# A selective scan on one core: the B product of four states at a time, decays in SBUF, and one session of activation functions per pass

## The chip, the cores and the metric

The kernel runs on one core of a Trainium2 chip. The core has five engines that run side by side, each working through its own queue in order: PE (TensorE, matrix products into PSUM), DVE (VectorE), ACT (ScalarE, activation functions), POOL (GpSimd) and SP (SyncE, which here issues DMAs). SBUF is the working memory, PSUM the memory that PE writes into; PSUM has eight banks of 512 fp32 values per partition. The metric is the device time of one execution in microseconds (us). It was 14339.09 us before the change (median of three runs, 14334.58 to 14341.66).

## The reference

The input is 16 images of 64 x 64 positions with 128 channels. Two layers follow each other, each as `x = x + layer(group_norm(x))`. Layer 0 is a two-dimensional LSTM over the diagonals of the image. Layer 1, in which the change lies, is a selective scan (Mamba) over the 4096 positions of each image, once forward and once backward, with the two results added:

```python
xz = x @ in_w.T
xc, z = jnp.split(xz, 2, axis=-1)             # 256 inner channels each
...
xc = jax.nn.silu(...)                         # after a causal convolution of 4 taps
dbl = xc @ x_w.T
dt, Bm, Cm = jnp.split(dbl, [DT_RANK, DT_RANK + D_STATE], axis=-1)
dt = jax.nn.softplus(dt @ dt_w.T + dt_b)
dA = jnp.exp(dt[..., None] * A)               # decay, 16 states per channel
dBx = dt[..., None] * Bm[:, :, None, :] * xc[..., None]
def step(h, inp):
    dA_t, dBx_t, C_t = inp
    h = dA_t * h + dBx_t
    y = jnp.einsum('bds,bs->bd', h, C_t)
    return (h, y)
...
y = ys + xc * D
y = y * jax.nn.silu(z)
return y @ out_w.T
```

For every inner channel and each of 16 states there is a recurrence over time, `h = decay * h + drive`, where the drive is `dt * x * B`; the output is the sum over the states of `h * C`.

## The kernel before

**Tiling.** Layer 1 works in 256 passes: 16 images, and for each 8 chunks of 512 positions forward and the same 8 backward. In a pass the 256 inner channels are two halves (`h` = 0, 1) of 128 partitions, and there are 16 states (`s`), so a pass has 32 recurrences of 512 steps. Each is one `tensor_tensor_scan` on DVE (line 1277, `scan`), with the decay as one tensor input, the drive as the other, and the last column of the chunk before (`carry`) as its start.

**Two ways for the states.** States 0 to 7 (kind "X" in the planner) get their drive from POOL: `drive` multiplies `dtx` = dt * x by a row of B that a DMA has spread over all partitions (`br`), for two states at once, into a tile `group` in SBUF that holds four states interleaved. The scan writes its result in place. PE then transposes the group (`turned`), ACT copies it out of PSUM (`turned_take`, into `ht`), and PE weighs it with C by a matrix product (`weigh`, with four column groups of 32). States 8 to 15 (kind "R") get their drive from PE: `drive_rows` multiplies the transposed `dtx` (`dtxt`) by a matrix `d` in which the B values of the states lie on a diagonal. That matrix is put together in DRAM by `scatter` and loaded by `spread`. The product of two states fills the two PSUM banks of the tile "pair", and the scan reads it from there and writes to `hst` in SBUF. POOL multiplies `hst` by a row of C (`out_of`, line 1300, into `hc`), and PE adds the result into the PSUM tile `py` (`sums`).

**Decays.** `decay` (line 1217) is an Exp on ACT. For the R states it writes to `das`, a tile of SBUF for two states; for the X states it writes to one of four PSUM banks, tag "bank0" to "bank3", which it shares with small products ("misc"). The planner limits each of the two uses to two banks at a time.

**PSUM.** The eight banks are: four of "bank", two of "pair" (also used by `dtproj`, the product for dt), two of "py".

**Activation functions.** Exp, Silu and Softplus need different tables on ACT, and a change of function needs a table load. In a pass ACT leaves Exp twice: for a session of Silu (of pass i + 2, and the gate of pass i in the backward passes) and for a session of Softplus (of pass i + 1). In a session no decay is issued between its activations.

**Order.** The order of all instructions is fixed ahead of the launch: `order_of_issue` lists every step with its engine, its cost (`COST`), what it must follow, what buffers it takes (`RINGS`) and a priority (`URGENCY`), and `simulate` plays this through and puts out one order. Each engine then runs its part in that order; waits between engines are by semaphores. `ORDER` says how scans of X groups (digits) and R pairs (letters) follow each other: "00a00b11c11d..." is two scans of group 0, two of pair a, two of group 0, two of pair b, and so on.

Of the kernel before, what the change touches and what calls it, by code (L numbers as in the profile page):

```python
# [8 lines left out]
F32 = mybir.dt.float32  # L9
# [5 lines left out]
P = 128  # L15
# [21 lines left out]
GX = 4  # L37
TB = P // GX
NX = 8
NG, NR = NX // GX, (NS - NX) // 2  # L40
WD = T + P
ORDER = ("00a00b11c11d22e22f33g33h", "00a00b11c11d22e22f33g33h")


def units_of(order):

    count = {}
    for x in order:
# [3 lines left out]
        else:  # L52
# [4 lines left out]
    "bank": 4, "pair": 1, "py": 1, "das": 3, "dg": 3, "group": 3, "cd": 2, "ht": 6, "hst": 3, "hc": 4,  # L57
    "br": 3, "cr": 2, "xc": 2, "dt": 2, "dtx": 2, "dtxt": 2, "dbl": 2, "z": 1, "y": 1,
# [4 lines left out]
    "conv": 0.865, "gate": 0.87, "silu": 0.62, "softplus": 0.65, "gate_take": 0.6, "dtproj": 1.07,  # L63
    "xproj": 1.0, "xproj_take": 0.4, "times": 2.34,
    "turn": 0.47, "turn_take": 0.47, "decay": 0.62, "drive": 2.34, "drive_rows": 1.08,
    "scan": 1.18, "keep": 0.6, "keep_group": 0.6, "out": 2.34, "sums": 0.88, "skip": 0.44,
    "turned": 0.44, "turned_take": 0.47, "weigh": 1.08,
    "again": 0.88, "finish": 1.0, "finish_last": 1.2, "back": 0.47, "back_take": 0.47,
    "project": 0.95, "store_take": 0.6, "residual": 0.6, "read_load": 0.6, "read_turn": 0.47,
    "read_take": 0.5, "read_stats": 0.62, "normal": 3.0, "normalise": 0.75, "spread": 0.6, "rows": 1.2,  # L70
# [4 lines left out]
LIMIT = {"misc": 2, "bank": 2}  # L75
AHEAD = 3
ROW = 0.9
# [4 lines left out]
        {(0, 0): -5.27, (0, 1): -61.96, (0, 2): -1.51, (0, 3): -31.9, (1, 0): -36.36, (1, 1): -34.22, (1,  # L82
         2): -4.82, (1, 3): -3.48},
        {(0, 0): -13, (0, 1): -15.31, (0, 2): -17.47, (0, 3): -12.25, (1, 0): -17.78, (1, 1): -17.99, (1,
         2): -18.46, (1, 3): -13.31},
    ),
    "xproj": (
        {(): 55.58},
        {(): 50.35},
    ),  # L90
    "xproj_take": (
        {(): -34.19},
        {(): -67.81},
    ),
    "rows": (
        {(): 14.85},
        {(): 29.35},
    ),
    "dtproj": (
        {(): 21.81},  # L100
        {(): 49.19},
    ),
    "times": (
        {(): -216.85},
        {(): -50.5},
    ),
    "turn": (
        {(0,): -139.83, (1,): -112.3},
        {(0,): 38.45, (1,): 39.27},
    ),  # L110
    "turn_take": (
        {(0,): -82.61, (1,): -85.08},
        {(0,): -121.61, (1,): -124.32},
    ),
    "skip": (
        {(0,): -30.72, (1,): -29.27, (2,): -28.89, (3,): -30.37},
        {(0,): -31.71, (1,): -38.35, (2,): -27.4, (3,): -32.33},
    ),
    "spread": (
        {("b", 0): 48.76, ("d", 0): -27.02, ("c", 0): -72.82, ("b", 1): -39.91, ("k", 0): 25.29, ("d",  # L120
         1): -25.84, ("c", 1): 91.24, ("b", 2): 203.69, ("d", 2): 42.8, ("c", 2): -76.57, ("b", 3): 83.9,
         ("k", 1): -178.37, ("d", 3): 47.98, ("c", 3): -120.82},
        {("b", 0): -102.07, ("d", 0): 101.39, ("c", 0): -127.37, ("b", 1): 201.12, ("k", 0): -7.75, ("d",
         1): -16.19, ("c", 1): 237.63, ("b", 2): 27.93, ("d", 2): 187.94, ("c", 2): 178.25, ("b", 3):
         59.58, ("k", 1): 33.49, ("d", 3): -19.86, ("c", 3): 49.53},
    ),
    "drive": (
        {(0, 0): -37.87, (1, 0): -232.55, (0, 1): 70.61, (1, 1): 81.52, (2, 0): 92.85, (3, 0): -81.77,
         (2, 1): 90.65, (3, 1): -60.19},
        {(0, 0): 71.45, (1, 0): 100.65, (0, 1): 69.84, (1, 1): 238.34, (2, 0): -85.16, (3, 0): 16.29, (2,  # L130
         1): 152.24, (3, 1): 151.41},
    ),
    "decay": (
        {(0, 0): -100.09, (1, 0): -113.38, (8, 0): -17.88, (9, 0): -17.98, (2, 0): 115.94, (3, 0):
         -173.37, (8, 1): 117.83, (9, 1): 117.76, (0, 1): 117.57, (1, 1): -199.13, (10, 0): -76.99, (11,
         0): -4.35, (2, 1): -207.87, (3, 1): -174.5, (10, 1): -57.93, (11, 1): 144.9, (4, 0): -62.8, (5,
         0): 9.44, (12, 0): -249.7, (13, 0): -4.82, (6, 0): -90.12, (7, 0): -89, (12, 1): 112.66, (13,
         1): -89.33, (4, 1): -92.07, (5, 1): -92.07, (14, 0): -87.45, (15, 0): -79.99, (6, 1): -83.78,
         (7, 1): -65.02, (14, 1): -92.12, (15, 1): -92.18},
        {(0, 0): -107.74, (1, 0): 78.08, (8, 0): 64.21, (9, 0): 60.4, (2, 0): 66.94, (3, 0): -168.8, (8,  # L140
         1): -38.24, (9, 1): 83.45, (0, 1): -165.22, (1, 1): -93.49, (10, 0): -104.1, (11, 0): 17.18, (2,
         1): 7.23, (3, 1): -108.8, (10, 1): 238.21, (11, 1): -142.57, (4, 0): 16.12, (5, 0): 79.59, (12,
         0): 187.77, (13, 0): -57.05, (6, 0): 11.51, (7, 0): -45.79, (12, 1): 48.63, (13, 1): 3.55, (4,
         1): 76.92, (5, 1): 79.55, (14, 0): 84.29, (15, 0): -45.77, (6, 1): 8.28, (7, 1): 1.52, (14, 1):
         78.29, (15, 1): 80.29},
    ),
    "scan": (
        {(0, 0): -191.9, (1, 0): -180.93, (8, 0): 59.29, (9, 0): 58.95, (2, 0): 47.07, (3, 0): 1.2, (8,
         1): 43.31, (9, 1): 42.72, (0, 1): 139.84, (1, 1): 85.46, (10, 0): 88.15, (11, 0): -220.11, (2,
         1): 67.38, (3, 1): 69.08, (10, 1): 3.2, (11, 1): -48.38, (4, 0): -148.38, (5, 0): -142.6, (12,  # L150
         0): -158.76, (13, 0): -146.42, (6, 0): -147.36, (7, 0): -134.74, (12, 1): -175.53, (13, 1):
         71.17, (4, 1): 33.69, (5, 1): 137.17, (14, 0): 92.55, (15, 0): 96.04, (6, 1): 94.32, (7, 1):
         102.78, (14, 1): 86.19, (15, 1): 71.66},
        {(0, 0): -48.3, (1, 0): -50.57, (8, 0): -47.99, (9, 0): -52.26, (2, 0): -45.52, (3, 0): -48.53,
         (8, 1): -128.37, (9, 1): -157.26, (0, 1): -63.33, (1, 1): -80.02, (10, 0): -74.43, (11, 0):
         -109.52, (2, 1): -66.59, (3, 1): -80.53, (10, 1): 9.22, (11, 1): -125.5, (4, 0): -93.94, (5, 0):
         3.58, (12, 0): 2.78, (13, 0): -27.3, (6, 0): 34.58, (7, 0): 18.59, (12, 1): 6.11, (13, 1):
         12.29, (4, 1): 11.19, (5, 1): 13.36, (14, 0): 20.12, (15, 0): 47.53, (6, 1): 63.73, (7, 1):
         24.81, (14, 1): -31.39, (15, 1): -31.89},
    ),  # L160
    "scatter": (
        {("d", 0): -127.75, ("k", 0): -48.3, ("d", 1): 125.59, ("d", 2): 30.9, ("k", 1): -11.07, ("d",
         3): 59.14},
        {("d", 0): -28.6, ("k", 0): -67.41, ("d", 1): -108.16, ("d", 2): -133.73, ("k", 1): -94.37, ("d",
         3): -129.9},
    ),
    "drive_rows": (
        {(0, 0): 26.17, (0, 1): -3.25, (1, 0): -50.93, (1, 1): -31.58, (2, 0): -0.9, (2, 1): 17.32, (3,
         0): 80.19, (3, 1): -2.75},
        {(0, 0): 33.35, (0, 1): 87.4, (1, 0): -31.34, (1, 1): 14.65, (2, 0): 33.69, (2, 1): 74.37, (3,  # L170
         0): 149.93, (3, 1): -83.5},
    ),
    "keep": (
        {(0, 0): -27.42, (0, 1): -63.13, (1, 0): -50.2, (1, 1): 26.86, (2, 0): 11.68, (2, 1): 92.99, (3,
         0): -130.98, (3, 1): -233.75},
        {(0, 0): -235.44, (0, 1): 51.58, (1, 0): 122.52, (1, 1): 76.67, (2, 0): 102.66, (2, 1): -10.28,
         (3, 0): 48.92, (3, 1): -97.12},
    ),
    "out_of": (
        {(0, 0): 59.79, (0, 1): 61.42, (1, 0): -184.01, (1, 1): -237.54, (2, 0): -19.88, (2, 1): -39.04,  # L180
         (3, 0): 15.92, (3, 1): -83.32},
        {(0, 0): 46.75, (0, 1): 3.87, (1, 0): 82.21, (1, 1): 206.76, (2, 0): 148, (2, 1): -37.11, (3, 0):
         94.4, (3, 1): 76.66},
    ),
    "sums": (
        {(0, 0): 41.95, (0, 1): 68.64, (1, 0): 88.31, (1, 1): 50.57, (2, 0): 73.72, (2, 1): 76.8, (3, 0):
         -112.6, (3, 1): 161.24},
        {(0, 0): 22.75, (0, 1): 60.23, (1, 0): 33.88, (1, 1): 40.44, (2, 0): 217.19, (2, 1): 108.14, (3,
         0): 79.41, (3, 1): 83.91},
    ),  # L190
    "keep_group": (
        {(0, 0): -57.74, (0, 1): 14.03, (1, 0): 44.89, (1, 1): 61.89},
        {(0, 0): -23.9, (0, 1): -25.46, (1, 0): -99.2, (1, 1): -131.55},
    ),
    "turned": (
        {(0, 0, 0): 7.49, (0, 0, 1): -48.32, (0, 0, 2): -49.41, (0, 0, 3): 27.18, (0, 1, 0): 30.12, (0,
         1, 1): 23.21, (0, 1, 2): 38.21, (0, 1, 3): 37.84, (1, 0, 0): 60.1, (1, 0, 1): 19.71, (1, 0, 2):
         91.82, (1, 0, 3): -28.89, (1, 1, 0): 50.64, (1, 1, 1): 50.33, (1, 1, 2): 64.2, (1, 1, 3): 154.68},
# [16 lines left out]
        {(0, 0): 103.15, (0, 1): 79.93, (1, 0): 103.9, (1, 1): 79.84},  # L215
    ),
    "finish": (
        {(): -99.64},
        {(): -37.02},
    ),  # L220
    "spill": (
# [1250 lines left out]
```

## Time and profile before

| | |
|---|---|
| median of 3 runs | 14339.09 us |
| the profiled execution | 14002.73 us |
| its span, first to last instruction | 14000.9 us |
| mean granted PE clock | 0.973 |
| busy, share of the span: PE | 13085.1 us, 93% |
| PE's weight loads | 10060.3 us, 72% |
| DVE | 11100.8 us, 79% |
| ACT | 10791.8 us, 77% |
| POOL | 10438.0 us, 75% |
| moved by DMA | 1936.50 MB, mean 138 GB/s |

All times of single rows come from the profiled execution, which was shorter than the median of the runs by 336 us. The span has two parts: layer 0, some 1.6 ms at the beginning, in which POOL does little, and layer 1, which repeats its pass to the end. The page also divides the span into 40 slices and shows the busy share of each engine in tenths:

```profile
PE   8999899898999999998989999998989999998989
DVE  6776678787887878787878888787878888787878
ACT  3444678788888878787888888788888888787877
POOL 0111488788878888887878888888878888888888
```

The first four digits are layer 0; from the fifth on, no engine's row changes much, so any stretch from there to the end stands for the rest. In the rows of the groups of instructions, which come with the prediction, the form is: line, engine, operation, output <- inputs, shapes, count, then busy time in us and the mean of one in ns, then the engine's idle time just before these instructions and what ended most of it.

### The profile page before, as it was taken

What the parts mean: (1) busy time and instruction counts of PE and PEld (TensorE: products, weight loads), DVE (VectorE), ACT (ScalarE), POOL (GpSimd) and SP (SyncE); (2) the same over time, 40 slices, a digit from 0 to 9 for tenths busy, and PEclk for the clock granted to TensorE, in tenths of its full rate; (3) what the DMA queues carried; (4) which work ended last, traced back from release to release, by engine and by line L of the source; (5) the groups of instructions that cost most, each with busy time, mean ns of one, the idle gap of its engine ahead of it and who ended that gap; (6) DMA issues with size and microseconds to landing.
All of it is one profiled execution on the core that took longest, in us unless ns stands there. A gap on an engine that the chain in (4) does not pass through costs nothing. (4 is left out here: it accounts for less than half of the span.)

```text
span 14000.9 us, 315690 instructions
## 1 busy us (share of the span) xinstructions
PE 13085.1 (93%) x124724; PEld 10060.3 (72%) x124724; DVE 11100.8 (79%) x11281; ACT 10791.8 (77%) x17599; POOL 10438.0 (75%) x4612
## 2 busy tenths in 40 slices
PE   8999899898999999998989999998989999998989
PEld 7666667676767777676767777776767677776767
DVE  6776678787887878787878888787878888787878
ACT  3444678788888878787888888788888888787877
POOL 0111488788878888887878888888878888888888
PEclk9999899999999999999999999999999999999999
DMA  4221356565555556565655555565655556565655
GB/s 144 56 57 51 84 144 156 137 152 141 152 146 147 149 144 152 137 156 141 152 142 150 149 146 147 143 158 141 151 144 153 144 149 146 143 156 142 152 141 140
DMA packets 3787992, 1936.50 MB, mean 138 GB/s; under 512 B 2938624, under 2 KB 3284240, under 8 KB 3786512
## 3 DMA queue, kind: packets, MB, share of 16 engines
q1 hardware_dynamic: 3708560, 1881.06, 53.2%
q10 hardware_dynamic: 77952, 35.24, 1.1%
q8 instruction: 986, 16.15, 0.5%
q14 instruction: 494, 4.05, 0.1%
HBM read 1754.87 MB, written 164.89 MB: 137 GB/s over the span
## 5 line engine op out<-in xcount | busy, mean ns | idle before, releaser
L1300 POOL TENSOR_TENSOR hc<-hst,cr 128x1024 f32<-128x1024 f32 x2048 | 4872.9, 2384 | 1497.8 <-DMA cr<-rows 1017.3
L1277 DVE TENSOR_TENSOR_SCAN hst<-das,carry,hps 128x512 f32<-128x512 f32 x3584 | 4376.8, 1262 | 1308.0 <-PE hps L1257 837.8
L1225 POOL TENSOR_TENSOR group<-dtx,br 128x1024 f32<-128x1024 f32 x2048 | 4898.5, 2406 | 403.3 <-DMA br<-rows 251.2
L1277 DVE TENSOR_TENSOR_SCAN group<-da,carry,group 128x512 f32<-128x512 f32 x3584 | 4393.1, 1263 | 463.9 <-ACT da L1217 324.2
L1217 ACT ACTIVATE das<-dt,A_log_sb 128x512 f32<-128x512 f32 x4096 | 2852.3, 724 | 744.5 <-DVE hst L1277 720.8
L1315 ACT COPY ht<-ptg 128x512 f32<-128x512 f32 x4096 | 2263.4, 588 | 890.9 <-PE ptg L1307 868.4
L1217 ACT ACTIVATE da<-dt,A_log_sb 128x512 f32<-128x512 f32 x4096 | 2766.5, 688 | 72.7 <-DVE group L1277 66.5
L1335 PE MATMUL py<-ident,hc 128*128 128x128 f32 x16384 | 2162.0, 281 | 495.7 <-POOL hc L1300 495.1
L1307 PE MATMUL ptg<-ident,group 128*128 128x128 f32 x16384 | 2415.1, 283 | 178.8 <-ACT ht L1315 153.6
L1257 PEld LDWEIGHTS hps<-d,dtxt 64*128 64x128 f32 x32768 | 2050.7, 192 | 636.6 <-issue 486.6
L1257 PE MATMUL hps<-d,dtxt 64*128 64x128 f32 x32768 | 2448.2, 290 | 21.8 <-ACT dt L1182 12.1
L1335 PEld LDWEIGHTS py<-ident,hc 128*128 128x128 f32 x16384 | 1869.3, 144 | 808.3 <-POOL hc L1300 532.5
L1307 PEld LDWEIGHTS ptg<-ident,group 128*128 128x128 f32 x16384 | 1820.5, 143 | 584.4 <-ACT ht L1315 252.5
L1093 PE MATMUL pp<-xT,wk 128*128 128x512 f32 x4096 | 1930.1, 609 | 0.5 <-DVE xl L880 0.5
L1093 PEld LDWEIGHTS pp<-xT,wk 128*128 128x128 f32 x4096 | 733.8, 192 | 735.1 <-issue 688.9
L859 POOL TENSOR_TENSOR a_f<-a_f,c 128x288 f32<-128x288 f32 (+40 forms) x254 | 212.7, 837 | 1331.0 <-ACT a_f L851 1265.9
L1323 PE MATMUL py<-ht,k 128*32 128x128 f32 x32768 | 1114.5, 277 | 0.3 <-ACT ht L1315 0.3
L1323 PEld LDWEIGHTS py<-ht,k 128*32 128x32 f32 x32768 | 837.4, 110 | 197.5 <-issue 177.4
L1191 POOL TENSOR_TENSOR dtx<-dt,xc 128x1024 f32<-128x1024 f32 x256 | 604.1, 2360 | 318.8 <-ACT dt L1182 291.0
L1277 DVE TENSOR_TENSOR_SCAN hst<-das,hps 128x512 f32<-128x512 f32 x512 | 595.4, 1201 | 237.0 <-PE hps L1257 201.2
L1217 ACT ACT_TABLE_LOAD x527 | 676.1, 1283 | 10.2 <-DVE hst L1277 0.4
L1277 DVE TENSOR_TENSOR_SCAN group<-da,group 128x512 f32<-128x512 f32 x512 | 596.0, 1202 | 68.9 <-ACT da L1217 63.7
(110 smaller groups left out, 11834.4 us busy)
## 6 DMA issues: line engine op xcount, KB each, us to landing
cr<-rows SPq DMA_DIRECT2D x1024, 512.0 KB
br<-rows SPq DMA_DIRECT2D x1024, 512.0 KB
d<-d SPq DMA_DIRECT2D x1024, 320.0 KB
k<-k SPq DMA_DIRECT2D x512, 256.0 KB
yf<-yo SPq DMA_DIRECT2D x128, 512.0 KB
yl<-yf SPq DMA_DIRECT2D x128, 512.0 KB
xs<-in_x_dram SPq DMA_DIRECT2D x64, 512.0 KB
d<-rows SPq DMA_DIRECT2D x2048, 2.0 KB
```

The costliest lines, as they stand in the source:

```text
L859: nc.gpsimd.tensor_mul(f0, f0, cp[:, up, :])
L1093: nc.tensor.matmul(self.ps["conv", h], lhsT=wk[:, k, h * P : (h + 1) * P], rhs=xT[self.b % 2][:, t0 : t0 + T], start=(k == 0), stop=(k == ...
L1191: nc.gpsimd.tensor_mul(self.dtx, self.dt, self.xc)
L1217: nc.scalar.activation(t, self.dt[:, h, :], AF.Exp, scale=amat[:, h, s : s + 1])
L1225: nc.gpsimd.tensor_mul(both[:, m : m + 2, :], bc(self.dtx[:, h, :], 1, 2), self.brow[q])
L1257: nc.tensor.matmul(half[:, j, :, :], lhsT=self.dtxt[rows, j, h * P : (h + 1) * P], rhs=dg[rows, j + r, :, :], start=True, stop=True, skip_ ...
L1277: nc.vector.tensor_tensor_scan(t[:, self.rev], self.da.pop((s, h))[:, self.rev], dbx[:, self.rev], 0.0 if self.first else carry[:, self.d, ...
L1300: nc.gpsimd.tensor_mul(self.hc[g, h], self.hst[g, h], self.crow[g])
L1307: nc.tensor.transpose(pt[:, k, :], self.group[g, h][:, t0 : t0 + TB, :].rearrange("p t s -> p (t s)"), ident,)
L1315: nc.scalar.copy(t, self.ps.pop(("turned", g, h, j)))
L1323: nc.tensor.matmul(self.py[q * TB : (q + 1) * TB, j // 2, c0 : c0 + P], lhsT=cd[:, GX * j + q, :], rhs=self.ht[g, h, j][:, q, :], start=False,
L1335: nc.tensor.matmul(self.py[:, j, cols], start=j not in self.banks, stop=last, skip_group_check=True, **how,)
```

## The change

**Four states in one B product.** The matrix `d` now holds four states and is 896 wide in place of 640 (`WD = T + 3 * P`); there are two of them a pass in place of four (`NA`). `drive_rows` cuts the 128 rows into four row groups of 32 instead of two of 64, and each group writes its own PSUM bank. The tile is called "quad" and has four banks; `dtproj` uses it too. `ORDER` puts four R scans in a row: "00aaaa0011bbbb1122cccc2233dddd33". POOL's `out_of` and the DMA that keeps the last column still go by pairs of states.

**Decays in SBUF.** To make room, all decays go to a ring "da" of eight SBUF tiles of one state each; "das" and the PSUM place for X decays are gone, and two banks are left for "misc". Decays are issued in the order of the scans.

**One session.** Silu of pass i + 2, the gate of pass i and Softplus of pass i + 1 form one session of ACT.

**The planner.** `COST` and `URGENCY` have new values throughout, a table `LINK` gives each kind of DMA its own cost, and the rings change: `hc` 4 to 3, `cr` 2 to 3, `dg` 3 to 2.

```diff
-WD = T + P
-ORDER = ("00a00b11c11d22e22f33g33h", "00a00b11c11d22e22f33g33h")
+WD = T + 3 * P
+ORDER = ("00aaaa0011bbbb1122cccc2233dddd33", "00aaaa0011bbbb1122cccc2233dddd33")
...
-    "bank": 4, "pair": 1, "py": 1, "das": 3, "dg": 3, "group": 3, "cd": 2, "ht": 6, "hst": 3, "hc": 4,
-    "br": 3, "cr": 2, "xc": 2, "dt": 2, "dtx": 2, "dtxt": 2, "dbl": 2, "z": 1, "y": 1,
+    "bank": 2, "quad": 1, "py": 1, "da": 8, "dg": 2, "group": 3, "cd": 2, "ht": 6, "hst": 3, "hc": 3,
+    "br": 3, "cr": 3, "xc": 2, "dt": 2, "dtx": 2, "dtxt": 2, "dbl": 2, "z": 1, "y": 1,
...
-        for part, q, size, (name, who, args, need, table) in [
-            (part, q, len(todo), x) for part, todo in enumerate((first, last)) for q, x in enumerate(todo)
-        ]:
+        for q, (name, who, args, need, table) in enumerate(first + last):
...
-            def decay(self, s, h, place=None):
-                if s >= NX:
-                    g, m = divmod(s - NX, 2)
-                    if m == 0:
-                        self.das[g, h] = ring(sp, "das", [P, 2, T], f"das_{self.nm}_{g}_{h}")
-                    t = self.das[g, h][:, m, :]
-                else:
-                    t = bank(place, f"da_{self.nm}_{s}_{h}")
+            def decay(self, s, h):
+                t = ring(sp, "da", [P, T], f"da_{self.nm}_{s}_{h}")
                 nc.scalar.activation(t, self.dt[:, h, :], AF.Exp, scale=amat[:, h, s : s + 1])
...
-                    for k in range(2):
-                        dst = bass.AP(t.tensor, t.offset + k, [[WD + 2, P], [P, NB]])
+                    for k in range(GX):
+                        dst = bass.AP(t.tensor, t.offset + k, [[WD + GX, P], [P, NB]])
...
-                step = P // NQ
-                dg = self.mat["d", g].rearrange("p (j i n) -> p j i n", n=2, i=step)
-                pair = psum.tile([P, NQ, T], F32, name=f"hps_{self.nm}_{g}_{h}", tag="pair")
+                dg = self.mat["d", a].rearrange("p (j i n) -> p j i n", n=GX, i=TB)
+                quad = psum.tile([P, GX, T], F32, name=f"hps_{self.nm}_{a}_{h}", tag="quad")
                 for j in range(NB):
-                    for r in range(NQ):
-                        rows = slice(r * step, (r + 1) * step)
-                        half = pair[:, r, :].rearrange("p (i j n) -> p j i n", j=NB, n=2)
+                    for r in range(GX):
+                        rows = slice(r * TB, (r + 1) * TB)
+                        part = quad[:, r, :].rearrange("p (i j n) -> p j i n", j=NB, n=GX)
                         nc.tensor.matmul(
-                            half[:, j, :, :],
+                            part[:, j, :, :],
                             lhsT=self.dtxt[rows, j, h * P : (h + 1) * P],
                             rhs=dg[rows, j + r, :, :],
```

## The prediction

> **What bounds the kernel now.** I read three views in this order: busy time in a stretch of layer 1, the groups of instructions, and the order of time. The columns of the first are the stretch, its length, and for each engine busy time and number of instructions.
>
> ```profile
> core 0: us, PE busy (x) PEld busy (x) DVE busy (x) ACT busy (x) POOL busy (x), PEclk, DMA share, GB/s
> 4000.00:12000.00 8000.00, 7469.98 (x75899) 5794.22 (x75898) 6477.39 (x5572) 6546.00 (x10360) 6583.55 (x2803) 0.98 0.59 147
> ```
>
> A pass of layer 1 has 17 POOL products (eight of `drive`, eight of `out_of`, one of `times`), so 2803 / 17 = 164.9 passes lie in 8000 us: **48.5 us a pass**. Per pass POOL is busy 6583.55 / 164.9 = 39.9 us, DVE 39.3, ACT 39.7, PE 45.3. No engine is full. PE stands nearest, but it is busy and not at its peak; DVE and POOL are two nearly equal loads that must overlap almost perfectly.
>
> ```profile
> L1300 POOL TENSOR_TENSOR hc<-hst,cr 128x1024 f32<-128x1024 f32 x2048 | 4872.9, 2384 | 1497.8 <-DMA cr<-rows 1017.3
> L1277 DVE TENSOR_TENSOR_SCAN hst<-das,carry,hps 128x512 f32<-128x512 f32 x3584 | 4376.8, 1262 | 1308.0 <-PE hps L1257 837.8
> L1225 POOL TENSOR_TENSOR group<-dtx,br 128x1024 f32<-128x1024 f32 x2048 | 4898.5, 2406 | 403.3 <-DMA br<-rows 251.2
> L1277 DVE TENSOR_TENSOR_SCAN group<-da,carry,group 128x512 f32<-128x512 f32 x3584 | 4393.1, 1263 | 463.9 <-ACT da L1217 324.2
> L1217 ACT ACTIVATE das<-dt,A_log_sb 128x512 f32<-128x512 f32 x4096 | 2852.3, 724 | 744.5 <-DVE hst L1277 720.8
> L1217 ACT ACTIVATE da<-dt,A_log_sb 128x512 f32<-128x512 f32 x4096 | 2766.5, 688 | 72.7 <-DVE group L1277 66.5
> L1257 PE MATMUL hps<-d,dtxt 64*128 64x128 f32 x32768 | 2448.2, 290 | 21.8 <-ACT dt L1182 12.1
> L1323 PE MATMUL py<-ht,k 128*32 128x128 f32 x32768 | 1114.5, 277 | 0.3 <-ACT ht L1315 0.3
> ```
>
> The largest DVE wait is for the B product of PE (`hps`). Both kinds of scan take 1.26 us though POOL works over 80% of the time beside them. What they share: **each has one SBUF tensor and one PSUM tensor**. The `hst` scan reads `das` (SBUF) and `hps` (PSUM); the `group` scan reads `da` (a PSUM bank) and `group` (SBUF). The third view is of layer 0, the one place where DVE products with two SBUF tensors meet POOL products (start, length, then the instruction):
>
> ```profile
> 355.35 0.96 POOL L859 TENSOR_TENSOR a_f<-a_f,c 128x368 f32<-128x368 f32 x1 [5.13 <-ACT a_f L851]
> ```
> ```profile
> 355.76 0.95 DVE L860 TENSOR_TENSOR a_f<-a_f,c 128x368 f32<-128x368 f32 x1 [2.64 <-ACT a_f L851]
> 356.81 0.54 DVE L862 TENSOR_TENSOR a_f<-a_f,a_f 128x368 f32<-128x368 f32 x1
> ```
>
> L860 and L862 are products of the same size, with both inputs in SBUF. Alone L862 takes 0.54 us. L860, started 0.41 us into the POOL product, takes 0.95 and ends 0.40 us after POOL does (356.71 against 356.31): it stood still until POOL was done, and saved only its start-up of 0.14 us. It goes the other way too: a POOL product of 144 elements at 1212.53 started inside L830 (end 1212.84) and took 0.66 us, of which 0.35 came after that end; two unobstructed POOL products (1272 ns for 512 elements, 1000 for 384) give 2.13 ns an element and thus 0.49 us for 144.
>
> **The change, part by part.**
>
> *B product in four row groups.* Per pass 64 matmuls (128 records) before and after, each of 128 columns, but for four states in place of two. Two row groups at a time cost 2448.2 / 32768 = 75 ns a record; the nearest row for four groups, in the columns, is `weigh`: 1114.5 / 32768 = 34 ns. So PE's 9.6 us a pass becomes between 4.4 and 9.6; I take 4.4, the like-sized row. PE goes to about 40 us a pass. The buffer is filled four times a pass instead of eight, and four `group` scans (4.7 us) now lie between one quad's last reading and the next one's first, where two lay before: the wait for `hps` largely goes.
>
> *Decays in SBUF.* Each of the 16 `group` decays costs 724 - 688 = 36 ns more, 0.6 us of ACT a pass. ACT is 82% busy, and up to eight decays are held ready (9.4 us of scans): nothing on the path; uncovered, 0.6 us. **But the 16 `group` scans of a pass now read `da` and `group`, both in SBUF.** The ordinary reading of the scan rows would price this at nothing, since 1263 and 1262 ns are the same. The Trainium skill (SBUF — State Buffer, section Who interferes with whom) speaks against it: a VectorE instruction with two SBUF inputs and a GpSimd instruction that reads SBUF exclude each other for the whole instruction. The layer 0 rows agree for products; no row shows such a scan. By the scan rows alone the change gains; by the rule every `group` scan and every POOL product take turns. I take the rule, because both engines' stand-still is in this trace.
>
> Sum by the rule. After a release a scan needs 1.26 - 0.14 = 1.12 us and a POOL product 2.39 - 0.14 = 2.25. Lower bound: they only exclude each other, all else hides: 17 x 2.25 + 16 x 1.12 = 56.2 us a pass. Upper bound: one POOL product goes ahead of every `group` scan and POOL rests under the 16 `hst` scans: 16 x (2.25 + 1.12) + 16 x 1.175 + 1.2 (gate product, residual) = 73.9 (1.175 is the pitch of two back-to-back scans, 2.35 / 2). Between them, a pass lasts 18.8 + 17.9 + 1.2 + 2.25 n, with n the POOL products that stand ahead of `group` scans. Four `hst` scans in a row cover two POOL products, so at best 8 of 17 fall there and n = 9. In the order of issue of the changed kernel, behind each quad stand the second `out_of` of that quad and two or three of `drive`, `times` or a late `out_of`, all ready: up to 15 can fall among the `group` scans. I take n = 11, nearer the lower end, as DVE's stand-still itself lets POOL run ahead and then starve: 62.7 us, and 0.8 us for the pass seam, where POOL waits for `dt` (198.4 us in these 165 passes by the view of waits, 1.2 us a pass) and a longer pass hides only part. **63.5 us, 15.0 more than now.** Behind a scan that stands still wait `out_of`, the transposes of `group` on PE and the decays of the next buffers; they are late with it, not in addition.
>
> *One session.* ACT table loads are 527 + 256 + 255 in the page's groups (1283 ns each), four a pass; after, three: 1.28 us of ACT less, off the path. The session (two loads, six activations) shuts decays out for about 2.6 + 4 x 0.69 + 2 x 0.60 = 6.5 us plus the load back, 7.8 us, less than the 9.4 us of decays held; if that cover fails, up to 7.8 us a pass. Softplus now follows Silu at once, so a late `dtproj` holds up every decay queued behind the session; today it holds them up behind the second session only.
>
> *Transfers and buffers.* The matrices for the B product go from four of 320 KB to two of 448 KB a pass, eight scatters either way, so SP issues two loads fewer; `cr` gets a third buffer, `hc` loses one, `dg` one. The wait for `cr` (1017.3 us in the page, 4 us a pass) is today inside POOL's slack; in a 60 us pass it is hidden either way. Nothing is booked.
>
> **Total.** 256 passes x 15.0 = 3840 us on the profiled execution's 14002.73 (span 14000.9) gives 17843. The timed runs have a median of 14339.09, 336 above; I keep that distance: **18180 us**.
>
> **Rivals.**
>
> *A, the forecast* (0.64): turns taken, n between 9 and 13.5, pass 58 to 69 us: 14339 + 256 x (9.5 to 20.5) = 16770 to 19590.
>
> *B, the mildest form* (0.12): POOL fills the `hst` stretches and the two engines merely add up, 56.2 to 58 us: 16310 to 16770. For it: POOL runs ahead whenever DVE stands. Against: an `out_of` is ready only after its pair's second scan.
>
> *C, lock-step* (0.10): n of 15 or more, and PE and ACT queues, set out for other times, stall with it: 70 to 74 us, 19840 to 20870.
>
> *D, the other side* (0.11): a scan with two SBUF tensors does not exclude POOL. Its place is the `group` scans; it decides if they keep about 1.26 us. For it: a scan takes 1.26 us for 512 elements where a product of that size takes about 0.69 (the 687 ns residual add), so it reads at half the pace, and no scan of this trace shows the stand-still. Then PE's relief is what counts: 5.2 us of PE go, and of DVE's 9 idle us a pass the wait for `hps` (668 us in these 165 passes by the view of waits, 4.1 us) mostly goes. I give 3.2 us, as POOL at 39.9 plus its waits is next: 14339 - 820 = 13520.
>
> *E, it doesn't do what it says for the time* (0.03): no exclusion, but the pass seam (`dt`, `times`, first `drive`) sets the pass and the longer session eats the relief: within 0.5 us a pass, 14339 +/- 130.
>
> **How the numbers follow.** The time is A's. The range holds A and most of B and C: 15900 to 20500, D and E left out. A measurement can tell about 0.2% from no change. Faster 0.11 (D), same 0.02 and 0.01 of slower (E), slower 0.87 with A, B and C.
>
> **What would show it.** Right: `group` scans with a mean far above 1.26 us (about 1.26 + 11 x 2.25 / 16 = 2.8), `hst` scans unchanged, POOL's two products longer in the mean, by up to 16 x 1.12 / 17 = 1.1 us, and a first scan behind a POOL product that ends about 1.1 us after it. Also right or wrong by themselves: `hps` matmuls near 34 ns of busy time a record, table loads at three quarters, decays of one mean. The forecast is wrong if `group` scans keep 1.26 us; its size is wrong if n is far from 11.

## The result and the profile after

The changed kernel takes **17300.88 us** (median of four runs, 17292.27 to 17304.72), against 14340.38 us for the kernel before, measured beside it: a ratio of 1.2056, with a 95% interval from 1.2032 to 1.2080. Its profiled execution took 17298.85 us, span 17297.0.

The busy time in a stretch of layer 1, with the columns of before:

```profile
core 0: us, PE busy (x) PEld busy (x) DVE busy (x) ACT busy (x) POOL busy (x), PEclk, DMA share, GB/s
4000.00:14000.00 10000.00, 7332.13 (x75049) 5552.38 (x75042) 9548.28 (x5504) 6390.05 (x10077) 8117.20 (x2772) 0.87 0.45 110
```

2772 POOL products / 17 are 163.1 passes in 10000 us: **61.3 us a pass** where there were 48.5. DVE is busy 95% of it, 58.6 us a pass after 39.3, with the same number of instructions. POOL rises from 39.9 to 49.8 us. PE is no longer the fullest engine. The groups, from the page:

```profile
L1278 DVE TENSOR_TENSOR_SCAN group<-da,carry,group 128x512 f32<-128x512 f32 x3584 | 8729.4, 2490 | 1.0 <-ACT da L1218 1.0
L1301 POOL TENSOR_TENSOR hc<-hst,cr 128x1024 f32<-128x1024 f32 x2048 | 5685.5, 2785 | 1603.6 <-DVE hst L1278 1314.8
L1226 POOL TENSOR_TENSOR group<-dtx,br 128x1024 f32<-128x1024 f32 x2048 | 6447.7, 3169 | 440.6 <-PE ptg L1308 351.8
L1278 DVE TENSOR_TENSOR_SCAN hst<-da,carry,hps 128x512 f32<-128x512 f32 x3584 | 4276.4, 1251 | 581.8 <-PE hps L1258 278.2
L1218 ACT ACTIVATE da<-dt,A_log_sb 128x512 f32<-128x512 f32 x8192 | 5629.4, 724 | 2507.3 <-DVE group L1278 2093.5
L1258 PE MATMUL hps<-d,dtxt 32*128 32x128 f32 x32768 | 1414.5, 317 | 116.4 <-DVE hst L1278 101.5
L1324 PE MATMUL py<-ht,k 128*32 128x128 f32 x32768 | 1122.4, 278 | 4.3 <-ACT ht L1316 4.3
```

The two kinds of scan had the same mean before. Now the `hst` scan, with its drive in PSUM, has 1251 ns, and the `group` scan, with both tensors in SBUF, 2490. This is where the time is: the group's busy time grew from 4393.1 to 8729.4 us. The loss shows as *busy* time, and almost none of it as idle time before the scan (1.0 us): the profile counts an instruction that stands still as started. A reader who looks only at waits would find DVE full and nothing that holds it.

The order of time shows one such meeting (start, length, instruction), first POOL, then DVE:

```profile
9039.43 3.30 POOL L1226 TENSOR_TENSOR group<-dtx,br 128x1024 f32<-128x1024 f32 x1
9042.69 3.29 POOL L1226 TENSOR_TENSOR group<-dtx,br 128x1024 f32<-128x1024 f32 x1
```
```profile
9040.48 3.34 DVE L1278 TENSOR_TENSOR_SCAN group<-da,carry,group 128x512 f32<-128x512 f32 x1
```

The first product ends at 42.73. The scan, started at 40.48, ends 1.09 us after that, at 43.82. The next product, started at 42.69, ends 2.16 us after the scan, at 45.98. Each engine's instruction lasts as long as both together, because each spends the other's time waiting.

### The profile page after: what moved, and what is told of

Read it like the earlier page. It is cut to its first block, busy times and chain, and to the rows that moved or that the text cites. A ratio compares the mean times of both kernels' runs of the same rounds, so it can differ in the third digit from the quotient of the medians.

```text
span 17297.0 us, 315328 instructions
## 1 busy us (share of the span) xinstructions
PE 13014.6 (75%) x124724; PEld 9803.7 (57%) x124724; DVE 16076.7 (93%) x11281; ACT 10672.4 (62%) x17344; POOL 12963.9 (75%) x4612
## 5 line engine op out<-in xcount | busy, mean ns | idle before, releaser
L1278 DVE TENSOR_TENSOR_SCAN group<-da,carry,group 128x512 f32<-128x512 f32 x3584 | 8729.4, 2490 | 1.0 <-ACT da L1218 1.0
L1218 ACT ACTIVATE da<-dt,A_log_sb 128x512 f32<-128x512 f32 x8192 | 5629.4, 724 | 2507.3 <-DVE group L1278 2093.5
L1301 POOL TENSOR_TENSOR hc<-hst,cr 128x1024 f32<-128x1024 f32 x2048 | 5685.5, 2785 | 1603.6 <-DVE hst L1278 1314.8
L1226 POOL TENSOR_TENSOR group<-dtx,br 128x1024 f32<-128x1024 f32 x2048 | 6447.7, 3169 | 440.6 <-PE ptg L1308 351.8
L1278 DVE TENSOR_TENSOR_SCAN hst<-da,carry,hps 128x512 f32<-128x512 f32 x3584 | 4276.4, 1251 | 581.8 <-PE hps L1258 278.2
L1258 PE MATMUL hps<-d,dtxt 32*128 32x128 f32 x32768 | 1414.5, 317 | 116.4 <-DVE hst L1278 101.5
L1258 PEld LDWEIGHTS hps<-d,dtxt 32*128 32x128 f32 x32768 | 1194.9, 217 | 434.0 <-DVE hst L1278 182.2
L1278 DVE TENSOR_TENSOR_SCAN group<-da,group 128x512 f32<-128x512 f32 x512 | 1302.1, 2591 | 11.0 <-DMA k<-rows 11.0
L1120 PE MATMUL pz<-in_wT,xT 128*128 128x256 f32 x1024 | 430.9, 594 | 544.2 <-ACT xc L1111 544.2
L1336 PE MATMUL py<-ddiag,xc 128*128 128x128 f32 x4096 | 691.4, 310 | 0.1
```

Of the source, the lines that this page charges most:

```text
L1120: nc.tensor.matmul(pz[:, j, :], lhsT=xT[self.b % 2][:, t0 : t0 + P], rhs=in_wT[:, DI:], start=True, stop=True,)
L1218: nc.scalar.activation(t, self.dt[:, h, :], AF.Exp, scale=amat[:, h, s : s + 1])
L1226: nc.gpsimd.tensor_mul(both[:, m : m + 2, :], bc(self.dtx[:, h, :], 1, 2), self.brow[q])
L1258: nc.tensor.matmul(part[:, j, :, :], lhsT=self.dtxt[rows, j, h * P : (h + 1) * P], rhs=dg[rows, j + r, :, :], start=True, stop=True, skip_ ...
L1278: nc.vector.tensor_tensor_scan(t[:, self.rev], self.da.pop((s, h))[:, self.rev], dbx[:, self.rev], 0.0 if self.first else carry[:, self.d, ...
L1301: nc.gpsimd.tensor_mul(self.hc[g, h], self.hst[g, h], self.crow[g])
```

## The experiments

Theory 1 is the prediction's: a scan with two SBUF tensors and a POOL product that reads SBUF exclude each other, and this is the whole loss. Theory 2 puts the loss on the rest of the change: the order of four and four, the four-bank quad, the single session.

**One part alone, and half of it.** The kernel before, in its own order, with the X decays in two SBUF tiles; `place[1]` is a slot number, of which the planner hands out two as it hands out two banks:

```diff
                 else:
-                    t = bank(place, f"da_{self.nm}_{s}_{h}")
+                    t = sp.tile([P, T], F32, name=f"da_{self.nm}_{s}_{h}", tag=f"dax{place[1]}", bufs=1)
```

> The kernel before, with one part of the change alone: the decays of states 0 to 7 go to two SBUF tiles in place of PSUM banks; order, buffers of everything else and PE work stay. Theory 1 (a scan with two SBUF tensors and a POOL product exclude each other): as in the changed kernel about 11 of 16 group scans a pass stand still, each for 1.8 us on average, 39.3 + 19.7 us of DVE and 2 to 4 us of waits, 61 to 63 us a pass; ratio 1.19 to 1.25. Theory 2 (the loss comes from the rest: the new order, the four-bank quad, one session): within 1% of the kernel before, group scans at 1.26 us. Theory 3 (both share it): ratio 1.05 to 1.15.

For the second kernel the same only where `h == 0`.

> As the one before, but only the decays of the first half of the channels (8 of 16 group scans a pass) go to SBUF. Theory 1: about 5.5 scans a pass stand still for 1.8 us, 10 us of DVE; the 9 us that DVE is idle today absorb part, so 52 to 55 us a pass, ratio 1.07 to 1.13; the group scans of the other half keep 1.26 us. Theory 2: no change. If the loss were a matter of the first scan of a run of group scans and not of each, half of the scans would cost as much as all.

Measured: 17096.32 us for all, ratio 1.1919 (1.1901 to 1.1937), 60.5 us a pass; 15390.19 us for half, ratio 1.0727 (1.0709 to 1.0745), 53.9 us a pass. The groups of the first:

```profile
L1282 DVE TENSOR_TENSOR_SCAN group<-da,carry,group 128x512 f32<-128x512 f32 x3584 | 8668.6, 2458 | 34.0 <-ACT da L1222 27.3
L1282 DVE TENSOR_TENSOR_SCAN hst<-das,carry,hps 128x512 f32<-128x512 f32 x3584 | 4350.1, 1252 | 399.1 <-PE hps L1262 334.5
```

The place of one operand, and nothing else, makes 93% of the loss (2748 of 2960 us), with nearly the same mean of the scan (2458 against 2490). In a stretch of 8000 us, 9.9 `group` scans a pass took over 1.4 us, and 5.1 with half of the decays in SBUF: the number goes with the scans that have two SBUF tensors. The pass grows by 5.4 us for the first half and 6.6 for the second by the profiles: DVE's busy time grows by 8.9 and 9.5 us a pass, and 3.5 and 2.9 of that go into time in which DVE was idle. Theory 2 falls as an account of the loss.

**The pairs by themselves.** A small kernel with stretches of 24 instructions on each engine:

```python
def scan_ss(): nc.vector.tensor_tensor_scan(state, decay, drive[:, :, 1], 0.0, ALU.mult, ALU.add)
def scan_ps(): nc.vector.tensor_tensor_scan(state, bank, drive[:, :, 1], 0.0, ALU.mult, ALU.add)  # bank in PSUM
def p_mul():   nc.gpsimd.tensor_mul(pc, pa, pb)
def p_copy():  nc.gpsimd.tensor_copy(pc, pa)
def p_set():   nc.gpsimd.memset(pc, 0.0)
```

> No part of the reference is computed; the output is zeros. Thirteen stretches of 24 instructions on DVE, on POOL or on both, with nothing that orders the two engines inside a stretch: a scan of 512 with both tensors in SBUF, with the drive in PSUM, with the decay in PSUM, and a product of 512 with both in SBUF; on POOL a product of 1024 (reads two SBUF tensors), a copy (reads one), a memset (reads none). Theory 1: alone, all three scans take about 1.2 us; beside POOL products the scan with two SBUF tensors takes about 3.3 us and POOL about as much, one pair in 3.35 us, while the scans with one PSUM tensor keep 1.2 and POOL 2.4. Beside the copy it alternates too, beside the memset it does not. Theory 2 (only products exclude POOL, a scan reads at half the pace and leaves room): the scan keeps 1.2 us beside POOL and only the DVE product stands still.

In the order of time, six of its stretches. L45 is the scan with two SBUF tensors, L51 the one with its decay in PSUM; L57 is POOL's product, L60 its copy, L63 its memset. The first lines are each alone, then come the pairs:

```profile
10.04 30.16 DVE L45 TENSOR_TENSOR_SCAN state<-decay,drive 128x512 f32<-128x512 f32 x24
128.84 57.95 POOL L57 TENSOR_TENSOR pc<-pa,pb 128x1024 f32<-128x1024 f32 x24
...
238.53 75.29 DVE L45 TENSOR_TENSOR_SCAN state<-decay,drive 128x512 f32<-128x512 f32 x24
239.69 76.27 POOL L57 TENSOR_TENSOR pc<-pa,pb 128x1024 f32<-128x1024 f32 x24
...
374.69 30.16 DVE L51 TENSOR_TENSOR_SCAN state<-bank,drive 128x512 f32<-128x512 f32 x24
374.98 58.24 POOL L57 TENSOR_TENSOR pc<-pa,pb 128x1024 f32<-128x1024 f32 x24
...
509.07 45.27 DVE L45 TENSOR_TENSOR_SCAN state<-decay,drive 128x512 f32<-128x512 f32 x24
510.21 44.96 POOL L60 COPY pc<-pa 128x1024 f32<-128x1024 f32 x24
...
555.41 30.17 DVE L45 TENSOR_TENSOR_SCAN state<-decay,drive 128x512 f32<-128x512 f32 x24
556.54 24.17 POOL L63 MEMSET pc<- 128x1024 f32 x24
```

The scan and the product alternate, one pair in 3.2 us: 1.08 for the scan after POOL's end, 2.13 for POOL after the scan's. With one operand in PSUM both run at the pace they have alone, whichever operand it is (the stretch with the drive in PSUM took 30.06 us beside 57.97). One SBUF input on POOL's side is enough to exclude (24 copies alone 26.30 us, here 44.96), and a memset, which reads nothing, does not. This is theory 1. Theory 2 of the expectation, a scan that leaves POOL room, is out.

**The rest of the change without the exclusion.** To see what the rest is worth, POOL's products were replaced, in both kernels, by something of about the same length that reads almost no SBUF:

```diff
-                nc.gpsimd.tensor_mul(self.hc[g, h], self.hst[g, h], self.crow[g])
+                part(self.hc[g, h], self.hst[g, h], self.crow[g])
...
+        def part(to, left, right):
+            few = slice(0, 8)
+            nc.gpsimd.tensor_mul(to[:, :, few], left[:, :, few], right[:, :, few])
+            for end in (T, T, 136):
+                nc.gpsimd.memset(to[:, :, 8:end], 0.01)
```

> The kernel before, with each POOL product (drive, out_of, times) computed for 8 of its 512 columns only; the rest of the tile is filled by memsets of about the same length (0.95 us for 1024 elements, so two whole ones and one of 128 columns a state), which read no SBUF. What is left out: the drive, the weighing by C and dt * x in 504 of 512 columns. POOL waits for the same tiles as before. Both theories: within 3% of the kernel before, as no group scan here has two SBUF tensors; it is the base for the next one.

> The changed kernel with the same filling in place of the POOL products (the same part of the computation left out). Its group scans have two SBUF tensors, but POOL reads almost none. Theory 1 (the whole loss is the exclusion): group scans go back to about 1.26 us, and against the filled kernel before it gains what the prediction's form D gave, about 6% (13500 us); anything from 0.93 to 1.00. If a good part of the loss came from the order, the four-bank quad or the single session, it stays above 1.03 of the filled kernel before with group scans at 1.26 us. If group scans stay long, the reading of POOL is not what excludes them.

This pair missed: 17752.70 us and 17718.37 us, nearly equal because POOL, busy 90% and 92% of 8000 us, was the fullest engine of both. A memset of the interleaved `group` tile took 1.96 us instead of 0.94, so a `drive` lasted 4.7 us. One thing it did show: the `group` scans of the second, both tensors in SBUF, kept 1267 ns. With the filling cut for `group` to `(T, 44)`:

> As s1_before_fill, with the filling cut to the length of a product: s1 showed that a memset of the group tile takes 1.96 us, twice that of the other tiles, so drive was 4.7 us long and POOL bound both filled kernels. Left out, as there: all but 8 of 512 columns of the drive, of dt * x and of the weighing by C. Both theories: within 4% of the kernel before, group scans at 1.26 us.

> The changed kernel with the same shorter filling, the same part left out. Theory 1 (the whole loss is the exclusion): group scans at about 1.26 us though both their tensors are in SBUF, and 0.93 to 1.00 of s3_before_fill. If the order, the four-bank quad or the single session cost something by themselves: above 1.01 of it. Against the kernel before the ratio is then 0.9 to 1.04, not 1.21.

Measured: 14369.38 us for the kernel before, ratio 1.0021 (1.0013 to 1.0030), so the filling stands in well for the products; 14525.64 us for the changed one, ratio 1.0140 (1.0124 to 1.0155). The `group` scans are back at 1267 ns with both tensors in SBUF, and all but 1.4% of the 20.6% is gone:

```profile
L1284 DVE TENSOR_TENSOR_SCAN group<-da,carry,group 128x512 f32<-128x512 f32 x3584 | 4323.5, 1267 | 5.5 <-ACT da L1224 5.2
```

But **the rest of the change brings nothing: 1.1% above the filled kernel before.** The same 1.1% lies between the changed kernel and the kernel before with its decays in SBUF (1.2056 / 1.1919). The view of waits over 8000 us says why; the kernel before, then the changed one (engine, line, who is waited for: us, times, longest):

```profile
DVE hst L1283 <- PE hps L1263: 625.8, 285, 7.1
DVE group L1283 <- ACT da L1223: 259.5, 163, 8.4
DVE hst L1283 <- DMA carry<-hst: 222.2, 77, 6.2
```
```profile
DVE hst L1284 <- DMA carry<-hst: 968.9, 131, 10.6
DVE hst L1284 <- ACT da L1224: 307.4, 106, 5.0
DVE hst L1284 <- POOL hc L1080: 194.5, 65, 9.2
DVE hst L1284 <- PE hps L1264: 178.2, 51, 9.9
```

The wait for the B product falls from 625.8 to 178.2 us, but a new one takes its place: the R scans, now four in a row, wait 968.9 us for the DMA that carries the last column of the chunk before. To test that, the DMA was replaced by a DVE copy of two or four columns, issued one scan later:

```diff
+                if kept:
+                    nc.vector.tensor_copy(*kept.pop())
+                if s >= NX and (s - NX) % 2:
+                    kept.append((carry[:, self.d, h, s - 1 : s + 1], self.hst[(s - NX) // 2, h][:, :, self.last]))
...
             def keep(self, g, h):
-
-                s = NX + 2 * g
-                nc.sync.dma_start(carry[:, self.d, h, s : s + 2], self.hst[g, h][:, :, self.last])
+                pass
```

> As s4_after_fill (the changed kernel, POOL products filled by memsets, the same part left out), and the last columns of the scans are carried over by a small DVE copy one scan later in place of a DMA. In s4 the wait of hst scans for carry was 969 us in 8000, where s3_before_fill had 222, and the wait for hps 178 where it had 626. If the four-state product did relieve the path and the carry DMA, held up in SP's queue, took the relief back: 2 to 5% less than s4, so below s3_before_fill (1.002 of the kernel before). If the pass is set by something else (Softplus behind dtproj, 760 us of ACT waits in s4): within 1% of s4, with the wait turned to another name.

Measured: 13707.45 us, ratio 0.9567 (0.9554 to 0.9580), 5.6% below the filled kernel with the DMA. The wait for the carry is gone, and the wait for the B product is back, longer than in the filled kernel before:

```profile
DVE hst L1284 <- PE hps L1264: 973.8, 295, 15.1
```

So the fall to 178.2 us was no relief that the four-state product gave by itself: without the wait for the carry, DVE waits for the product again. The gain of 5.6% comes from taking the carry DMAs out, and in two ways that this run doesn't separate: the R scans don't wait for them, and SP, which issues its DMAs in order, doesn't stand still for them (in 8000 us it stood 1446.3 us behind `hst` scans before such DMAs in the changed filled kernel, 671.1 in the other). Whether the filled kernel before would gain from the same copy was not tried, so the 4.5% to that one is not a measure of the four-state product alone.

**The single session.** The kernel before with a third `cr` buffer and one session, priorities searched anew by playing the order through with costs as profiled; and, to read it against, the same buffer and search with two sessions:

```diff
-            (part, q, len(todo), x) for part, todo in enumerate((first, last)) for q, x in enumerate(todo)
+            (0, q, len(first + last), x) for q, x in enumerate(first + last)
```

> The kernel before with one session of Silu, gate and Softplus a pass, decays of states 0 to 7 still in PSUM and pairs of states as before; a third buffer for cr, costs as the profile shows them and priorities searched anew for this structure (the old ones were set for two sessions). To be read against c2_replanned. Table loads fall from four to three a pass. If the single session costs or gains nothing: within 1% of c2_replanned. If it is a part of the loss: 2% or more above.

> The kernel before with a third buffer for cr, costs as the profile shows them and priorities searched anew; every group scan keeps one tensor in PSUM. If the waits at the seam of the passes (dt, hps, br) are a matter of the order: 2 to 5% faster than the kernel before and no slower than c1_third_cr (0.971); if they are set by PE's own work: as c1_third_cr.

Both missed: 15861.09 us, ratio 1.1075 (1.1058 to 1.1091), and 15210.65 us, ratio 1.0618 (1.0602 to 1.0634). Even the better one lies far above the next experiment, which has the same third buffer and the old order (0.9713). Between the two lie 4.3%, with table loads at 783 instead of 1038 a run, but two searches with different ends lie between them too. What the single session costs by itself stays open.

**Looking for a faster version.** The change's third `cr` buffer alone, in the kernel before:

```diff
-    "br": 3, "cr": 2, "xc": 2,
+    "br": 3, "cr": 3, "xc": 2,
```

> The kernel before with a third buffer for the rows of C (as the changed kernel has), the order unchanged. The wait of out_of for cr, 1017 us in the profile before, may shrink. If that wait sets the pass, up to 2% faster; if it is POOL's slack, within 0.3%.

> c1_third_cr with the same DVE copies in place of the carry DMAs (12 a pass, about 0.1 us of DVE each); order unchanged. In c1 the hst scans waited 257 us in 8000 for carry, and SP's queue stood 751 us behind scans before it could issue the next loads. If these count: 1 to 3% less than c1_third_cr, ratio 0.94 to 0.96. If DVE's 1.2 us a pass of copies cost what they save: 0.97 to 0.98.

The third buffer gives **13903.46 us, ratio 0.9713 (0.9699 to 0.9728), faster than both kernels**, and by more than the 2% that was thought the most. The idle time before POOL's `hc` product fell from 1497.8 to 458.6 us:

```profile
L1225 POOL TENSOR_TENSOR group<-dtx,br 128x1024 f32<-128x1024 f32 x2048 | 4899.8, 2407 | 975.0 <-DMA br<-rows 802.1
...
L1300 POOL TENSOR_TENSOR hc<-hst,cr 128x1024 f32<-128x1024 f32 x2048 | 4877.6, 2387 | 458.6 <-DVE hst L1277 302.4
```

Most of it came back one product further, before `group` (403.3 to 975.0) and `dtx` (318.8 to 683.1); the three together fall by 103 us, about what the spans of the two profiles differ by (98 us). The rest of the gain in the timed runs is taken up in the last section.

The DVE copy for the carry, which had helped the filled kernel, did the opposite here: 15400.66 us, ratio 1.0746 (1.0731 to 1.0760). The order of time shows the copy of two elements, which takes 0.13 us at its shortest:

```profile
7999.51 2.37 POOL L1304 TENSOR_TENSOR hc<-hst,cr 128x1024 f32<-128x1024 f32 x1 [1.33 <-issue]
```
```profile
8000.47 1.44 DVE L1286 COPY carry<-hst 128x2 f32<-128x2 f32 x1
```

It ends at 8001.91, right after POOL's 8001.88. A DVE copy from SBUF to SBUF is one more instruction that POOL shuts out; these copies have a mean of 1.06 us, and there are 12 a pass. The scan behind a copy starts 1.30 us after it in the median, so DVE stands with it: DVE's busy time rises from 39.2 to 50.7 us a pass, against the third buffer alone, and the idle time there, 8.9 us, takes up only part. In the filled kernel the next scan started 0.05 us after the copy in the median, and DVE's busy time rose by only 0.9 us a pass.

## Why the prediction was right

**The mechanism was right.** It came from the row of layer 0 and from the rule of the Trainium skill that the prediction names, and the trace of after agrees with both. `group` scans were foretold at about 2.8 us and have 2.49 to 2.59; `hst` scans are unchanged; the tail after POOL's end was foretold at 1.1 us and has a median of 1.08. The rival without exclusion, D, is out: it gave 13520 us and `group` scans of 1.26.

**The number of scans that stand still, n, was right:** taken as 11, it is 11.0 of 16 a pass (scans over 1.4 us in the stretch of 10000 us). In the runs of four `group` scans behind a quad mostly three stand still (303 of 651) or four (166), for `out_of` (5.1 a pass), `drive` (5.5) and now and then `times` (0.4). That supports the argument that an `out_of` and some further products stand ready there, at the low end of its count. The argument gave 9 to 15, and 11 was picked from it by judgement; that it met the count so closely is luck.

**The price of one was too high.** The sum booked a whole POOL product, 2.25 us, ahead of each. The trace has 19.7 us a pass of excess over 11.0 scans, 1.79 us each, as a scan often starts when part of the product is done. This term was mis-sized: it is 24.75 - 19.7 = 5.0 us a pass too large. The stand-alone terms were good: 1.12 foretold against 1.08 for the scan, 2.25 against 2.13 for the product. On the other side the sum left only 0.8 us for other waits, where DVE is idle 2.8 us a pass, and it took 17.9 + 18.8 + 1.2 us for work that took 58.6 - 19.7 = 38.9. These 2.0 and 1.0 us too little offset more than half of the 5.0 too much, so that the sum came to 63.5, with 61.3 measured, is in part luck too.

**The base was off.** The prediction set its 15.0 us on top of a profiled execution that was 336 us shorter than the timed runs, and kept that distance for after, where it is 2 us. Between the timed runs a pass grew by (17300.88 - 14340.38) / 256 = 11.6 us. Of the 879 us by which 18180 lay too high, the pass makes (63.5 - 61.35) x 256 = 550, with 61.35 us from one `times` to the next, and the distance, 336 - 2, makes the rest but for 5 us. The time lies inside the range and inside form A.

**The smaller parts.** Decays have one mean, 724 ns, as foretold. Table loads are 272 + 256 + 255, three quarters of 1038. POOL's products grew by 0.40 us (`hc`) and 0.76 us (`group`), under the bound of 1.1. The `hps` matmuls cost 1414.5 / 32768 = 43 ns a record, between the two rows, where 34 was taken; in the filled kernel they cost 37.

**The wait for `hps`** went as foretold (668 us in 8000 of before, 182 in 10000 of after). That it went for the reason given, the four `group` scans between two quads, is not shown. With the decays in SBUF and pairs as before, the idle time of `hst` scans for `hps` already fell from 837.8 to 334.5 us over the whole run, where the pass is longer too; and with quads, but without the exclusion and the carry DMA, DVE waited 973.8 us in 8000. **Wrong was what would come next if it went:** form D named POOL with its waits, and the filled kernels showed the carry DMA and, on ACT, Softplus behind `dtproj` (760 us in 8000). By the filled kernels, D's gain of 820 us would not have come from this change even without the exclusion.

## What to carry to other kernels

On this chip, count SBUF tensors before moving an operand from PSUM: a DVE scan or product with two, or a small DVE copy from SBUF to SBUF, takes turns with a POOL instruction that reads SBUF, and for the scan one operand in PSUM makes the two independent. The cost shows as a longer mean of both engines' instructions and not as a wait, so look at the spread of durations of one shape, not at idle time. A relieved wait is worth only the distance to the next one: ask which DMA or session stands behind it before booking the gain.

## What the runs showed of the hardware

- A DVE copy of two or four elements is shut out for up to 2.4 us by a POOL product (mean 1.06 us, shortest 0.13), and the next scan with it. In the filled kernel such copies were long in the trace too (mean 0.88 us): of 851 that began inside a POOL memset of 1008 elements, nearly all ended 0.02 to 0.03 us after it. But there the next scan did not wait for the copy, and a memset did not hold up a scan with two SBUF tensors.
- A DVE product of 512 whose second input has a step of four elements took 26.34 / 24 = 1.10 us alone. The residual add of 512 elements, without such a step but with one input in PSUM, takes 0.69 in the kernel before; the step was not tried by itself.
- POOL's memset of 1008 elements took 0.94 us into a plain tile and 1.96 us into the interleaved `group` tile.
- The profiled execution of before was 336 us (2.3%) shorter than the median of the timed runs of that kernel and 300 us shorter than the shortest of all (14302.33 us). Its granted PE clock was 0.973, where 43 timed runs with a clock on record had 0.963 to 0.966. Every other kernel's profile lay within 0.2% of its timed median. By the profiles the third `cr` buffer gains 0.7%, by the timed runs 2.9%. Why is open; there is only one profile of the kernel before.
- PE's granted clock was 0.97 in before, 0.93 with the decays in SBUF and 0.87 after, where PE was less busy (93, 82 and 75% of the span). In the last two DVE is the fullest engine (93%), and no run tells what sets the clock.
